# Where a transformer block's vector work is done: keys' weights scaled ahead, key and value blocks made by VectorE alone, and the second norm in two operations over more heads

## The chip, the cores and the metric

The kernel runs on one NeuronCore of a Trainium2 chip. The metric is the device time of one execution in microseconds (us), the median of several runs. A profile of one execution gives each instruction's start and length on TensorE (PE), VectorE (DVE), ScalarE (ACT), GpSimd (POOL) and on SyncE's DMA queue (SP).

## The reference

The program is one transformer block with conditioned layer norms (adaLN), on x of 4 batches x 512 tokens x 512 features, all in fp32:

```python
mod = (silu(c) @ wmod).reshape(4, 6, 1, -1)           # sa, ca, ga, sb, cb, gb
h = layernorm(x) * (1 + ca) + sa
q, k, v = h @ Wq + bq, h @ Wk + bk, h @ Wv + bv       # 16 heads of 128
w = softmax(q @ k.T / sqrt(128) + causal_mask)
x = x + ga * ((w @ v) @ Wo + bo)
h = layernorm(x) * (1 + cb) + sb
x = x + gb * (top2_of_8_experts(h) + shared_expert(h))
```

`ga` and `gb` are kept at least 0.25 away from zero. The change touches the keys and values, and the second layer norm.

## The kernel before, in words

**Products in seven.** The projections of queries, keys, values and the output are 2x2 block products done with seven block multiplications instead of eight (the generator `seven`, L531). Each product goes into a PSUM bank of tag "w", of which there are three, and is taken from there by the engine that the caller names: `p1` (the first product, copied), `11` and `12`, `21`, `22` (the four result blocks), and the running sums `u2`, `u3`, `u4`. If the caller gives a `p5`, the fifth product is first copied to SBUF and the rest works on the copy. The weights' block sums (three more blocks from the four, four additions) are made once, on GpSimd, in batch 0 (`sums_of_a` L505, `sums_of_b` L512) and kept in DRAM (`save_sums` L585). Later batches load two blocks from the input and five from the kept sums (L581, L582).

**Keys** (`project_k`, L654) carry the factor 128^-0.5. Each operation that leaves PSUM applies it. ScalarE takes p1 with the bias (L672), takes the product of u3 with a bias, and copies p5 (L689). GpSimd adds u3 (L679), 22 (L690) and u4 (L692). VectorE does u2, 11, 21 and 12 (all L675). There are 32 key blocks. **Values** (`project_v`, L701): ScalarE copies p1 (L724) and p5 (L727), GpSimd adds 22 (L728) and u4 (L732), VectorE does the rest (L725 to L734). There are 16. **Queries** (`project_q`, L615) take only p1 with ScalarE; all the rest is VectorE's, straight from the bank (L642 to L650).

**Attention.** The work is 16 groups (4 batches b x 4 groups g), four heads u each. In a head, `scores` (L791) makes four blocks of logits: TensorE the products, VectorE the mask (L804) and the negated maximum (L806), ScalarE the exponential (L808), VectorE the reciprocal sums (L812), ScalarE the scaling (L815). `attend` (L817) turns the probabilities with TensorE (L825), copies them out (VectorE L833, ScalarE L835), and multiplies with the values (L839). A head's `scores` are interleaved with the `attend` of the head before.

**The order is written out by hand** for TensorE, VectorE, ScalarE and SP (L1076); each executes in that order and waits where an operand isn't there. GpSimd's order is the planner's. `weave_at` (L1027) runs the eight steps k = 0 to 7 of a head, after each puts in as many steps of `fill` (keys, values, output products) as the head's plan says (L1056 to L1073), and after the steps named in `spots` one step of `side`:

```python
for k, n in enumerate(plan):
    next(main)
    for _ in range(n):
        next(fill)
    if k in spots:
        next(side)
```

**The second norm** (`second_norm`, L964) of batch b-1 is such a side, of 22 steps, run in the heads of batch b's first two groups: four steps of the residual (`xres * ga` on VectorE L234, `+ x` on GpSimd L235); four of statistics (L241, L242), the last with the inverse deviation; four of blocks (subtract and scale L259 on VectorE, `* rows[0]` L276 on VectorE, `+ rows[1]` L277 on GpSimd); then `route` (L308): four steps that turn the blocks with TensorE (L285) and make the router's logits, and six that choose the experts and scatter the rows to DRAM with indirect DMAs on GpSimd (L416). Spots (L1119 to L1125): g = 0: four steps in u1, eight in u2, four in u3; g = 1: three in u0, three in u1. In the last batch (`idle`) ScalarE makes the blocks (L268) after the attention.

**What shares its buffers.** `xres` (the residual and the output projection's sum) has one buffer: `open_out` (L865) fills it with the bias for the next batch at (g, u) = (0, 2), after its old contents went to `xr` in DRAM (L966). `xh` has one buffer: it holds x for the residual and then the second norm's blocks, until the scatter; `load_first` (L858) loads the next batch's x into it at (2, 0), and that batch's first norm (L241, L259) runs at g = 2, u = 2 and 3.

After attention come the shared expert and the routed experts, which the change leaves alone.

Of the kernel before, what the change touches and what calls it, by code (L numbers as in the profile page):

```python
# [8 lines left out]
F32 = mybir.dt.float32  # L9
AF = mybir.ActivationFunctionType  # L10
ALU = mybir.AluOpType
# [3 lines left out]
P = 128  # L15
# [35 lines left out]
def adaln_block_kernel(  # L51
# [64 lines left out]
    for i in range(NT):  # L116
# [26 lines left out]

    sums = {
        "wq": dram.tile([H // 2, P, 5 * 2 * DH], F32, name="sums_q"),
        "wk": dram.tile([H // 2, P, 5 * 2 * DH], F32, name="sums_k"),
        "wv": dram.tile([NG, P, 5 * 4 * DH], F32, name="sums_v"),
        "wo": dram.tile([NG, P, 2 * 6 * HW], F32, name="sums_o"),
        "ws": dram.tile([NSC, P, 7, 2, P], F32, name="sums_s"),
# [74 lines left out]
    def normed(b, n, fine=(1,)):  # L224


        if n == 1:
            src = xh = late["first"]
        else:
            src = xres[b]  # L230
            xh = late["x"]
            rows = late["mod"]
            for t in range(NTB):
                nc.vector.tensor_mul(src[:, t, :], src[:, t, :], ga_bc)  # L234
                nc.gpsimd.tensor_add(src[:, t, :], src[:, t, :], xh[:, t, :])  # L235
                yield
        idle = n == 2 and b == B - 1
        mv = small.tile([P, NTB, 2], F32, tag="mv", name=f"mv_{n}_{b}")
        for t in range(NTB):
            st = small.tile([P, 6], F32, tag="st", name=f"st_{n}_{b}_{t}")  # L240
            nc.vector.bn_stats(st, src[:, t, :])  # L241
            nc.vector.bn_aggr(mv[:, t, :], st)  # L242
            if t in fine:
                yield
        rstd = small.tile([P, NTB], F32, tag="rstd", name=f"rstd_{n}_{b}")
        nc.vector.tensor_scalar_add(rstd, mv[:, :, 1], EPS)
        if idle:
            load_lnexp()
        nc.scalar.activation(rstd, rstd, AF.Ln)
        nc.scalar.activation(rstd, rstd, AF.Exp, scale=-0.5)  # L250
        if idle:
            less = small.tile([P, NTB], F32, tag="less", name=f"less_{n}_{b}")
            nc.vector.scalar_tensor_tensor(
                less, mv[:, :, 0], -1.0, rstd, op0=ALU.mult, op1=ALU.mult
            )
        yield
        for t in range(NTB):
            if not idle:
                nc.vector.tensor_scalar(  # L259
                    xh[:, t, :],  # L260
                    src[:, t, :],
                    mv[:, t, 0:1],
                    rstd[:, t : t + 1],
                    op0=ALU.subtract,
                    op1=ALU.mult,
                )
            else:
                nc.scalar.activation(  # L268
                    xh[:, t, :],
                    src[:, t, :],  # L270
                    AF.Identity,
                    bias=less[:, t : t + 1],
                    scale=rstd[:, t : t + 1],
                )
            if n == 2:
                nc.vector.tensor_mul(xh[:, t, :], xh[:, t, :], rows[0])  # L276
                nc.gpsimd.tensor_add(xh[:, t, :], xh[:, t, :], rows[1])  # L277
            if t in fine:
                yield
        late[b] = xh  # L280
# [291 lines left out]

    def load_quadrants(tag, src, j, b, n=2 * DH, bufs=2):

        w = wts.tile([P, 7, 2, n // 2], F32, tag=tag, bufs=bufs, name=f"{tag}_{b}_{j}")
        flat = w.rearrange("p q c n -> p (q c n)")
        if b == 0:
            nc.sync.dma_start(out=flat[:, : 4 * n], in_=src[j])
            sums_of_a(nc.gpsimd, w)
        else:  # L580
            nc.sync.dma_start(out=flat[:, : 2 * n], in_=src[j, :, : 2 * n])  # L581
            nc.sync.dma_start(out=flat[:, 2 * n :], in_=sums[tag][j])  # L582
        return w

    def save_sums(tag, j, b, w):  # L585
        if b == 0:
            nc.sync.dma_start(
                out=sums[tag][j], in_=w[:, 2:].rearrange("p q c n -> p (q c n)")
            )

    def load_wq(b, j):
# [62 lines left out]
    def project_k(b, i, w, kT):  # L654


        def mm(k, dst):
            sa, sb_ = PROD[k]
            for c in range(2):
                nc.tensor.matmul(  # L660
                    dst,
                    lhsT=w[:, sa, c, :],
                    rhs=h7[b][:, sb_, c, :],
                    start=c == 0,
                    stop=c == 1,
                )

        def out(r, s):
            return kT[:, r, s * HW : (s + 1) * HW]

        def biased(o, p, bias):
            nc.scalar.activation(o, p, AF.Identity, bias=bias, scale=qscale)  # L672

        def add(o, p, u, scale=qscale):
            nc.vector.scalar_tensor_tensor(o, p, scale, u, op0=ALU.mult, op1=ALU.add)  # L675

        def u3(o, p, u):
            biased(o, p, dbk[:, i : i + 1])
            nc.gpsimd.tensor_add(o, o, u)  # L679

        yield from seven(
            f"k_{b}_{i}",
            HW,
            mm,
            {
                "p1": lambda o, p: biased(o, p, sbk[:, 2 * i : 2 * i + 1]),
                "u2": add,
                "u3": u3,
                "p5": lambda o, p: nc.scalar.mul(o, p, qscale),  # L689
                "22": lambda p5, u3: nc.gpsimd.tensor_add(out(1, 1), p5, u3),  # L690
                "21": lambda p, u3: add(out(1, 0), p, u3, -qscale),
                "u4": lambda o, p5, u2: nc.gpsimd.tensor_add(o, p5, u2),  # L692
                "11": lambda p, p1: add(out(0, 0), p, p1),
                "12": lambda p, u4: add(out(0, 1), p, u4),
            },
        )

# [3 lines left out]
    def project_v(b, g, w, v):  # L701


        def mm(k, dst):
            sa, sb_ = PROD[k]
            for t2 in range(2):
                for c in range(2):
                    nc.tensor.matmul(  # L708
                        dst[:, t2 * HW : (t2 + 1) * HW],
                        lhsT=h7[b][:, sb_, c, t2 * P : (t2 + 1) * P],  # L710
                        rhs=w[:, sa, c, :],
                        start=t2 == 0 and c == 0,
                        stop=t2 == 1 and c == 1,
                    )

        def out(r, s):
            return v[:, 2 * s : 2 * s + 2, r * HW : (r + 1) * HW]

        yield from seven(
            f"v_{b}_{g}",  # L720
            S,
            mm,
            {
                "p1": lambda o, p: nc.scalar.copy(o, p),  # L724
                "u2": lambda o, p, u: nc.vector.tensor_add(o, p, u),  # L725
                "u3": lambda o, p, u: nc.vector.tensor_add(o, p, u),
                "p5": lambda o, p: nc.scalar.copy(o, p),  # L727
                "22": lambda p5, u3: nc.gpsimd.tensor_add(  # L728
                    out(1, 1), halves(p5), halves(u3)
                ),  # L730
                "21": lambda p, u3: nc.vector.tensor_sub(out(1, 0), halves(u3), halves(p)),
                "u4": lambda o, p5, u2: nc.gpsimd.tensor_add(o, p5, u2),  # L732
                "11": lambda p, p1: nc.vector.tensor_add(out(0, 0), halves(p), halves(p1)),
                "12": lambda p, u4: nc.vector.tensor_add(out(0, 1), halves(p), halves(u4)),  # L734
            },
        )
# [226 lines left out]

    def second_norm(b):  # L964
        yield from normed(b, 2, (0, 1, 2))
        nc.sync.dma_start(out=xr[b], in_=xres[b].rearrange("p t d -> p (t d)"))  # L966
        yield
        yield from route(b, late[b])

# [106 lines left out]
    with tc.manual_schedule(engines={ENG.PE, ENG.DVE, ENG.Activation, ENG.SP}):  # L1076
# [18 lines left out]
        for G in range(NGB):  # L1095
# [14 lines left out]
            for u in range(GH):  # L1110
# [8 lines left out]
                if g == 0 and b > 0 and u > 0:  # L1119
                    if u == 1:  # L1120
                        second = side = second_norm(b - 1)
                    spots = range(8) if u == 2 else (1, 3, 5, 7)
                elif g == 1 and b > 0 and u < 2:
                    side = second
                    spots = ((1, 3, 5), (1, 3, 7))[u]  # L1125
                elif g == 2 and u >= 2 and b + 1 < B:
                    if u == 2:
                        side = in_order(normed(b + 1, 1))
                    spots = (1, 3)
                elif g == 3 and u == 2 and b + 1 < B:  # L1130
                    side = in_order(quadrants(b + 1))
                    spots = (0, 1, 3, 5)
# [26 lines left out]
                    next(prepare, None)  # L1159

                if b + 1 < B:
                    if (g, u) == (2, 0):
                        load_first(b + 1)
                if (g, u) == (0, 1):
                    wos[G] = load_wo(b, 0)
                if (g, u) == (0, 2 if b > 0 else 1):
                    open_out(b)
                if (g, u) == (3, 2):
                    load_for_second(b)
# [657 lines left out]
```

## Time and profile before

| | |
|---|---|
| runs | 1762.41, 1763.12, 1766.95 us; median 1763.12 |
| the profiled execution | 1764.14 us, span 1762.4 us |
| granted TensorE clock, mean of the span | 0.994 |
| attention and projections | up to about 1240 us of the span |
| DMA | 301.14 MB, mean 171 GB/s |

How to read it. A row of a group has the line, engine, operation, output <- inputs, shape, count, and after the bar busy us and mean ns. A row of waits has who waited for whom, then us in total, times, and the longest. A timeline row has start (us), length (us), engine, line, operation, tiles, shape, count; the bracket is the engine's idle time before it and what ended that. [...] A window row has its length, and then for PE, PEld (weight loads), DVE, ACT and POOL the busy us with the count of instructions, the granted TensorE clock, the share of the DMA engines and GB/s.

The page cuts the span into 40 slices of 44 us; its DMA line has the engines nearly full in batch 0 (from about 110 to 330 us):

```
DMA  5569989736343254334324275615324555565352
```

### The profile page before, as it was taken

Reading aid. Unit: us, or ns where it says so; the run is one execution under the profiler, and the core shown is the slowest. Engines: PE = TensorE matmul, PEld = TensorE weight load, DVE = VectorE, ACT = ScalarE, POOL = GpSimd, SP = SyncE. Lnnn points to the kernel's source line nnn. Section 1 sums busy time; section 2 is a strip of 40 time slices with the busy share of each in tenths; the row PEclk is TensorE's granted clock in tenths of the full one; section 3 lists DMA queues with packets and bytes.
Section 4 is the critical chain, followed back from the end, with each engine's and each line's share of the span. In section 5 each row is a group of like instructions: output and inputs, shape, how many; then the busy total and the mean of one; then the engine's idle time right before and its main releaser. Section 6 shows DMA issues by size and latency. Waiting matters only on the chain. (4 is left out here: it accounts for less than half of the span.)

```text
span 1762.4 us, 21698 instructions
## 1 busy us (share of the span) xinstructions
PE 1701.7 (97%) x7550; PEld 1302.2 (74%) x7550; DVE 896.5 (51%) x1891; ACT 528.5 (30%) x1298; POOL 589.5 (33%) x703
## 2 busy tenths in 40 slices
PE   6999999999999999999999989999999999999998
PEld 4767787787778888688788867787788565655687
DVE  4454454546545455754655475444776232121298
ACT  1025444303453420444441144444320111111120
POOL 6335553314354220525330255533620111000370
PEclk9999999999999999999999999999999999999999
DMA  5569989736343254334324275615324555565352
GB/s 219 184 213 303 281 291 301 261 116 239 94 166 112 84 168 146 124 108 142 110 101 146 96 253 180 196 55 227 126 94 169 215 191 170 193 215 186 110 182 68
DMA packets 158526, 301.14 MB, mean 171 GB/s; under 512 B 19136, under 2 KB 99008, under 8 KB 151760
## 3 DMA queue, kind: packets, MB, share of 16 engines
q1 hardware_dynamic: 153296, 282.96, 47.7%
q0 software_dynamic: 5120, 16.78, 2.9%
q8 instruction: 61, 1.00, 0.2%
q14 instruction: 49, 0.40, 0.1%
HBM read 247.25 MB, written 97.03 MB: 195 GB/s over the span
## 5 line engine op out<-in xcount | busy, mean ns | idle before, releaser
L808 ACT ACTIVATE prob<-ps,nmax 128x128 f32<-128x128 f32 (+3 forms) x256 | 134.4, 525 | 363.2 <-DVE nmax L806 355.6
L660 PE MATMUL w_k<-h,wk 128*128 128x256 f32 x896 | 223.5, 387 | 4.6 <-DVE h L515 2.4
L745 PE MATMUL w_o<-wo,oS 128*128 128x256 f32 x896 | 208.9, 379 | 0.0
L708 PE MATMUL w_v<-wv,h 128*128 128x256 f32 x896 | 206.0, 379 | 1.3 <-DVE u_q L642 1.3
L622 PE MATMUL w_q<-h,wq 128*128 128x256 f32 x896 | 201.9, 380 | 1.8 <-DVE qT L648 1.8
L622 PEld LDWEIGHTS w_q<-h,wq 128*128 128x128 f32 x896 | 168.7, 190 | 27.8 <-issue 3.4
L660 PEld LDWEIGHTS w_k<-h,wk 128*128 128x128 f32 x896 | 165.9, 195 | 27.9 <-ACT p_k L672 5.3
L708 PEld LDWEIGHTS w_v<-wv,h 128*128 128x128 f32 x896 | 167.4, 190 | 22.9 <-DVE u_q L642 1.7
L745 PEld LDWEIGHTS w_o<-wo,oS 128*128 128x128 f32 x896 | 164.6, 190 | 21.3 <-issue 1.4
L797 PE MATMUL ps<-kT,qT 128*128 128x128 f32 (+3 forms) x512 | 173.2, 440 | 1.4 <-ACT prob L808 1.4
L839 PE MATMUL po<-probT,v 128*128 128x512 f32 (+3 forms) x512 | 150.4, 435 | 12.3 <-DVE probT L833 12.3
L839 PEld LDWEIGHTS po<-probT,v 128*128 128x128 f32 x512 | 95.5, 190 | 68.7 <-issue 30.3
L815 ACT ACTIVATE prob<-prob,rsum 128x128 f32<-128x128 f32 (+3 forms) x256 | 122.8, 551 | 63.2 <-DVE rsum L812 61.5
L825 PEld LDWEIGHTS ppt<-ident,prob 128*128 128x128 f32 x640 | 83.3, 143 | 73.4 <-issue 34.7
L758 POOL TENSOR_TENSOR xres<-xres,p_o 128x512 f32<-128x512 f32 x48 | 61.4, 1281 | 209.4 <-DVE xres L758 118.1
L806 DVE TENSOR_REDUCE nmax<-ps 128x1 f32<-128x128 f32 (+3 forms) x256 | 125.7, 491 | 8.8
L1259 PE MATMUL w_s<-h2s,ws 128*128 128x256 f32 x560 | 124.4, 381 | 3.3 <-DVE hid L1245 1.8
L1259 PEld LDWEIGHTS w_s<-h2s,ws 128*128 128x128 f32 x560 | 105.0, 190 | 20.8 <-issue 2.7
L825 PE MATMUL ppt<-ident,prob 128*128 128x128 f32 x640 | 108.4, 278 | 7.6 <-ACT prob L815 5.1
L804 DVE TENSOR_TENSOR ps<-ps,cmask 128x128 f32<-128x128 f32 x256 | 75.1, 293 | 60.4 <-PE ps L797 52.2
L1516 PE MATMUL pyt<-wdn,hTt 128*128 128x512 f32 (+1 forms) x216 | 98.7, 593 | 0.0
L1499 DVE TENSOR_TENSOR ht<-tsg,put 128x352 f32<-128x352 f32 x36 | 18.8, 521 | 147.5 <-PE put L1489 123.0
(281 smaller groups left out, 2348.9 us busy)
## 6 DMA issues: line engine op xcount, KB each, us to landing
wgu<-in_wexp_dram SPq DMA_DIRECT2D x36, 1408.0 KB
xs<-nothing SPq DMA_DIRECT2D x15, 2304.0 KB
wdn<-in_wexp_dram SPq DMA_DIRECT2D x36, 768.0 KB
wo<-sums_o SPq DMA_DIRECT2D x12, 1536.0 KB
wq<-sums_q SPq DMA_DIRECT2D x24, 640.0 KB
wk<-sums_k SPq DMA_DIRECT2D x24, 640.0 KB
wv<-sums_v SPq DMA_DIRECT2D x12, 1280.0 KB
xt<-xs SPq DMA_DIRECT2D x36, 256.0 KB
```

The source lines that it names most:

```text
L622: nc.tensor.matmul(dst, lhsT=w[:, sa, c, :], rhs=h7[b][:, sb_, c, :], start=c == 0, stop=c == 1,)
L660: nc.tensor.matmul(dst, lhsT=w[:, sa, c, :], rhs=h7[b][:, sb_, c, :], start=c == 0, stop=c == 1,)
L708: nc.tensor.matmul(dst[:, t2 * HW : (t2 + 1) * HW], lhsT=h7[b][:, sb_, c, t2 * P : (t2 + 1) * P], rhs=w[:, sa, c, :], start=t2 == 0 and c ...
L745: nc.tensor.matmul(dst[:, t2 * HW : (t2 + 1) * HW], lhsT=oSs[hp][:, sa, t2 * P : (t2 + 1) * P], rhs=w[:, hp, sb_, :], start=t2 == 0 and hp ...
L797: nc.tensor.matmul(ps[:, :n], lhsT=qT[:, q0 : q0 + P], rhs=kT[:, u % 2, :n], start=True, stop=True,)
L806: nc.vector.tensor_reduce(nmax, ps[:, :n], AX.X, ALU.max, negate=True)
L808: nc.scalar.activation(blk, ps[:, :n], AF.Exp, bias=nmax, accum_out=rsum[:, i : i + 1])
L815: nc.scalar.mul(blk, blk, rsum[:, k : k + 1])
L825: nc.tensor.transpose(pt[:, at : at + P], prob[:, QO[i] + j * P : QO[i] + (j + 1) * P], ident,)
L839: nc.tensor.matmul(po[:, j * P :], lhsT=v()[:, j, u * DH : (u + 1) * DH], rhs=probT[:, KO[j] : KO[j] + (NTB - j) * P], start=(j == 0), sto ...
L1259: nc.tensor.matmul(dst[:, n * HW : (n + 1) * HW], lhsT=ws[k][:, sa, c, :], rhs=h2s[b + n][:, sb_, c, :], start=(n == 0 and c == 0), stop=( ...
L1516: nc.tensor.matmul(py, lhsT=hT_t[:fn, k, :], rhs=wdn[i % 2][:fn, k * D : (k + 1) * D], start=(k == 0), stop=(k == len(FCH) - 1),)
```

## The change

What it does:

- The keys' weights are multiplied by 128^-0.5 on GpSimd right after they are loaded in batch 0, ahead of their sums. All seven blocks are kept in DRAM (896 KB for 640 KB), and later batches load them in one DMA.
- Keys are then taken like queries: ScalarE only p1; u2, u3, 22, u4, 21, 11 and 12 on VectorE from the bank. Values have no p5 either: 22 and u4 are VectorE's.
- A block of the second norm (other than the last batch's) is two `scalar_tensor_tensor` on VectorE: (x - mean) * rows[0], then * rstd + rows[1].
- The 22 steps of the second norm are placed otherwise: g = 0: four in u1, two in u2, two in u3; g = 1: four, four, three, three in u0 to u3. The store to `xr` goes out right after the residual's fourth addition. `open_out` moves from (0, 2) to (1, 0), `load_first` from (2, 0) to (2, 1), and the first norm's steps in u2 from k = 1, 3 to k = 5, 7.

```diff
-        "wk": dram.tile([H // 2, P, 5 * 2 * DH], F32, name="sums_k"),
+        "wk": dram.tile([H // 2, P, 7 * 2 * DH], F32, name="sums_k"),
...
                 nc.gpsimd.tensor_add(src[:, t, :], src[:, t, :], xh[:, t, :])
+                if t == NTB - 1 and b < B - 1:
+                    nc.sync.dma_start(out=xr[b], in_=src.rearrange("p t d -> p (t d)"))
                 yield
...
-            if not idle:
+            if n == 1:
                 nc.vector.tensor_scalar(
...
+            elif not idle:
+                nc.vector.scalar_tensor_tensor(
+                    xh[:, t, :],
+                    src[:, t, :],
+                    mv[:, t, 0:1],
+                    rows[0],
+                    op0=ALU.subtract,
+                    op1=ALU.mult,
+                )
+                nc.vector.scalar_tensor_tensor(
+                    xh[:, t, :],
+                    xh[:, t, :],
+                    rstd[:, t : t + 1],
+                    rows[1],
+                    op0=ALU.mult,
+                    op1=ALU.add,
+                )
             else:
...
-            if n == 2:
                 nc.vector.tensor_mul(xh[:, t, :], xh[:, t, :], rows[0])
                 nc.gpsimd.tensor_add(xh[:, t, :], xh[:, t, :], rows[1])
...
             nc.sync.dma_start(out=flat[:, : 4 * n], in_=src[j])
+            if tag == "wk":
+                nc.gpsimd.tensor_scalar_mul(flat[:, : 4 * n], flat[:, : 4 * n], qscale)
             sums_of_a(nc.gpsimd, w)
+        elif tag == "wk":
+            nc.sync.dma_start(out=flat, in_=sums[tag][j])
...
-                "p1": lambda o, p: biased(o, p, sbk[:, 2 * i : 2 * i + 1]),
-                "u2": add,
-                "u3": u3,
-                "p5": lambda o, p: nc.scalar.mul(o, p, qscale),
-                "22": lambda p5, u3: nc.gpsimd.tensor_add(out(1, 1), p5, u3),
-                "21": lambda p, u3: add(out(1, 0), p, u3, -qscale),
-                "u4": lambda o, p5, u2: nc.gpsimd.tensor_add(o, p5, u2),
-                "11": lambda p, p1: add(out(0, 0), p, p1),
-                "12": lambda p, u4: add(out(0, 1), p, u4),
+                "p1": lambda o, p: nc.scalar.activation(o, p, AF.Identity, bias=bias),
+                "u2": lambda o, p, u: nc.vector.tensor_add(o, p, u),
+                "u3": lambda o, p, u: nc.vector.scalar_tensor_tensor(
+                    o, p, d, u, op0=ALU.add, op1=ALU.add
+                ),
+                "22": lambda p, u3: nc.vector.tensor_add(out(1, 1), p, u3),
+                "u4": lambda o, p, u2: nc.vector.tensor_add(o, p, u2),
+                "21": lambda p, u3: nc.vector.tensor_sub(out(1, 0), u3, p),
+                "11": lambda p, p1: nc.vector.tensor_add(out(0, 0), p, p1),
+                "12": lambda p, u4: nc.vector.tensor_add(out(0, 1), p, u4),
...
-                "p5": lambda o, p: nc.scalar.copy(o, p),
-                "22": lambda p5, u3: nc.gpsimd.tensor_add(
-                    out(1, 1), halves(p5), halves(u3)
-                ),
+                "22": lambda p, u3: nc.vector.tensor_add(out(1, 1), halves(p), halves(u3)),
...
-                "u4": lambda o, p5, u2: nc.gpsimd.tensor_add(o, p5, u2),
+                "u4": lambda o, p, u2: nc.vector.tensor_add(o, p, u2),
...
-                    spots = range(8) if u == 2 else (1, 3, 5, 7)
-                elif g == 1 and b > 0 and u < 2:
+                    spots = ((1, 3, 5, 7), (3, 7), (3, 7))[u - 1]
+                elif g == 1 and b > 0:
                     side = second
-                    spots = ((1, 3, 5), (1, 3, 7))[u]
+                    spots = ((1, 3, 5, 7), (1, 3, 5, 7), (1, 3, 5), (1, 3, 7))[u]
...
-                    spots = (1, 3)
+                    spots = ((5, 7), (1, 3))[u - 2]
...
-                    if (g, u) == (2, 0):
+                    if (g, u) == (2, 1):
                         load_first(b + 1)
...
-                if (g, u) == (0, 2 if b > 0 else 1):
+                if (g, u) == ((1, 0) if b > 0 else (0, 1)):
                     open_out(b)
```

## The prediction

> **What bounds the kernel now.** I read the page first, then TensorE's waits, then the timelines of the places where those waits sit, then clock by window, then mean durations by shape.
>
> ```profile
> PE 1701.7 (97%) x7550; PEld 1302.2 (74%) x7550; DVE 896.5 (51%) x1891; ACT 528.5 (30%) x1298; POOL 589.5 (33%) x703
> ```
>
> TensorE is busy 1701.7 of 1762.4 us. The change leaves its instructions alone, so all it can win is the 60.7 us of idle time plus matmuls that ran at a lower clock. TensorE's waits:
>
> ```profile
> PE po L839 <- DVE probT L833: 12.3, 6, 2.7
> PE pln L285 <- POOL xh L277: 5.5, 6, 1.6
> PE ppt L825 <- ACT prob L815: 5.1, 13, 1.5
> PE w_k L660 <- ACT p_k L672: 2.2, 5, 0.5
> ```
>
> TensorE's timeline puts most of these 30 gaps in a few places. Three times, once a batch, it looks like this (last batch; the bracket is the idle time before the row):
>
> ```profile
> 1031.39 0.92 PE L839 MATMUL po<-probT,v 128*128 128x256 f32 x4 [2.69 <-DVE probT L833]
> 1037.30 0.33 PE L285 MATMUL pln<-ident,xh 128*128 128x128 f32 x1 [0.16 <-POOL xh L277]
> 1039.19 0.36 PE L285 MATMUL pln<-ident,xh 128*128 128x128 f32 x1 [1.56 <-POOL xh L277]
> ```
>
> VectorE and GpSimd in that place:
>
> ```profile
> 1028.85 0.89 DVE L259 TENSOR_SCALAR xh<-xres,mv,rstd 128x512 f32<-128x512 f32 x1
> 1029.77 1.10 DVE L276 TENSOR_TENSOR xh<-xh,rows 128x512 f32<-128x512 f32 x1
> 1030.79 0.55 DVE L833 COPY probT<-ppt 128x384 f32<-128x384 f32 x1
> ...
> 1036.16 1.64 DVE L276 TENSOR_TENSOR xh<-xh,rows 128x512 f32<-128x512 f32 x1
> ...
> 1037.87 1.26 POOL L277 TENSOR_TENSOR xh<-xh,rows 128x512 f32<-128x512 f32 x1 [0.62 <-DVE xh L276]
> ```
>
> Eight steps of the second norm in one head (u2) put its statistics and blocks ahead of that head's transposed-probability copy (L833); VectorE is 98% busy in 1030 to 1040, TensorE 69%. The clock drops just there:
>
> ```profile
> 1020.00:1030.00 10.00, 8.63 (x40) 5.87 (x39) 9.10 (x25) 6.14 (x18) 5.63 (x6) 1.00 0.97 368
> 1030.00:1040.00 10.00, 6.89 (x26) 4.96 (x27) 9.75 (x15) 4.03 (x12) 8.04 (x8) 0.80 0.82 325
> 1040.00:1050.00 10.00, 10.00 (x57) 7.89 (x56) 3.29 (x9) 5.57 (x13) 6.16 (x9) 0.86 0.71 232
> ```
>
> The second place is the keys' block. GpSimd is in order, and the keys' additions queue behind whatever it has; VectorE waits for them, and the softmax behind VectorE:
>
> ```profile
> 209.84 0.73 POOL L690 TENSOR_TENSOR kT<-p_k,u_k 128x256 f32<-128x256 f32 x1
> 210.52 0.73 POOL L692 TENSOR_TENSOR p_k<-p_k,u_k 128x256 f32<-128x256 f32 x1
> ...
> 211.28 0.42 DVE L675 SCALAR_TENSOR_TENSOR kT<-w_k,p_k 128x256 f32<-128x256 f32 x1 [3.23 <-POOL p_k L692]
> 211.63 0.17 DVE L812 RECIPROCAL rsum<-rsum 128x4 f32<-128x4 f32 x1
> ...
> 211.83 1.92 ACT L815 ACTIVATE prob<-prob,rsum 128x128 f32<-128x128 f32 x4 [3.42 <-DVE rsum L812]
> ...
> 212.28 0.73 PE L825 MATMUL ppt<-ident,prob 128*128 128x128 f32 x2 [0.74 <-ACT prob L815]
> ```
>
> Here the keys' sums had waited behind four sums of wo (204.2 to 209.9).
>
> **Part 1: keys and values on VectorE.** GpSimd loses 24.6 + 24.2 + 23.4 us (keys: L692, L679, L690) and 20.3 + 20.3 (values: L732, L728). ScalarE loses 15.1 (u3) + 12.6 (p5) + 9.4 (values' p5) = 37 us. VectorE gains per key block what the queries' rows of the same shape cost: u3 0.48 (L643), u4 0.40 (L647), 22 about 0.42 = 1.30 us, x32 = 42 us; per value block 2 x 0.69 (L725) = 1.38, x16 = 22 us. The four key operations it had stay near 0.42. [...] The bank is held for two operations instead of one copy (0.8 for 0.4 us in keys); three banks rotate, product time 0.86 us, so it is covered.
>
> What falls away is GpSimd's delay. Gaps that the timeline ties to it: 1.88 at 143 us, 1.75 at 212 to 216, 2.63 at 271 to 277, 1.95 at 336 to 338, 1.76 at 1112: **10.0 us, of which I count 9** (some of ScalarE's softmax backlog stays). Next late there is ScalarE's p1, whose waits at 326, 626 and 922 (0.37 each) stay.
>
> **Part 2: scaling the keys' weights.** Eight GpSimd multiplications 128x1024, no row like it. Below: a memset 32x2048 took 1.80 us, so 0.9; above: twice the two-input 128x512 addition, 2.5. I take 1.7, 14 us in all. No PE wait names these sums. At the start two come before use: wk's sums ended at 17.0 us and TensorE needs them after 24.8; wq's ended at 25.6 and the first is needed at 35.4. Even 5 us later is covered. In batch 0 each save grows from 640 to 896 KB, 2.1 MB in all, 7 us of transfer at 295 GB/s where DMA is 99% busy. SP waits for it before reloading wk, but a reload issued at 212 is used some 45 us later. Zero; without cover, up to 7. Later batches load the same bytes in one DMA instead of two: nothing.
>
> **Part 3: the norm's block.** Before: L259 0.58 and L276 1.40 (0.69 free, 1.64 beside GpSimd's L277), then L277 1.41 on GpSimd. After: two operations of two SBUF tensors and a scalar. Bounds 0.69 (free) and 1.64 (contended); nearest row L1563, 0.75, so 1.5 us a block. VectorE saves 12 x 0.5 = 6 us, GpSimd 17, and the waits on L277 have no source left.
>
> **Part 4: the spreading.** The order of the 22 steps stays; head u2 gets 2 instead of 8, both statistics. Gone should be 6.5 us of waits for L833 (1.93 + 1.92 + 2.69), 5.5 for L277 and 0.9 of the transposes at 440: **12.9, I count 12**. The lower clock: 10 us windows at 0.83 (440), 0.98 and 0.85 (726, 736), 0.80 and 0.86 (1030, 1040) cost 1.7 + 1.7 + 3.4 = **6.8 us**. [...] The rows show the dips, but only where several gaps come within 10 us; the lone 1.9 to 2.1 us gaps at 143 and 271 have clock 1.00. As the gaps go, so should the dips: I take 6.8.
>
> New costs. (a) Head g1 u0 now holds a key block and four norm blocks. Nearest: the head at 858, with a key block and first-norm blocks (1.87 and 0.91 us of VectorE before the copy). Its L833 copy ended at 868.47, TensorE could use it from 869.19. The new head has 3.0 of norm for 2.78, 1.07 more of keys (start to start), less 0.41 that VectorE idled: 869.35, 0.2 late; with contended norm operations up to 3.5. I take 0.7 x 3 = 2. (b) The head at 858 itself gets 1.07: 0.5 x 3 = 1.5. (c) load_first one head later: SP now issues it behind wv (837.6). 1.8 + 1.0 MB at 300 GB/s land near 848; the statistics moved to about 854. Free, but in batch 0, where DMA is full and sums_o (1.5 MB) goes first, near 255 against 253.5; behind that wait stand rsum and the next masks: 1.5 (0 to 5). (d) Values' VectorE work beside the modulation rows (stalls at 62 and 110 us): 0.7. (e) xr's store, now ahead of wo on SP, waits for the last L235 (727): wo 4 us later, needed 50 us on; the bias load of xres at about 766 instead of 740, needed at 786: zero. The h2 stores queue after it. Route's steps in heads g1 u1 to u3: 0.3. Scatter's 8 us on GpSimd moves to g1 u3, after the output block instead of into it: zero. **Sum 6 us (0 to 17).**
>
> **The sum.** 9 + 12 + 6.8 - 6 = 21.8 us. The profiled execution took 1764.14 with span 1762.4, 1.7 outside; the median of the three runs is 1763.12. 1763.1 - 21.8 = 1741.3; I say 1742. VectorE should go to about 954 us (54%).
>
> **Rivals.** *The stall only moves*: cost (a) at its contended end, 3.5 x 3 = 10.5 instead of 2, and at most half of the clock term won. Then 21.8 - 8.5 - (3.4 to 6.8) = 6.5 to 9.9: 1753 to 1757. For it: that head is nearly full. Against: GpSimd has no norm or key work left there. *No change*: full DMA in batch 0 (7) and a late x (3.5 more) as well, and the boundaries' 12 us half won: within 5 of 1763. *VectorE becomes the bound*, which ends slower: it gets 64 us more work, in order, in heads where the softmax hangs on it. It decides where a block's additions push L833 past TensorE's second matmul on it, a margin of 0.7 us in the head at 858. If all 48 blocks do and TensorE loses 1.2 us on each (the 1.38 of a value block less fill), that is 58 us, less the 27.8 won: 1793. Against: a key head then has 3.0 + 4.5 us of VectorE work (softmax rows L804, L806, L812, L833) beside 12.8 of TensorE, so only bursts could do it. *The change doesn't act as said*: GpSimd, ordered by the planner, could put the multiplications ahead of L235, on which the statistics wait; at most 1.7 us each in batch 0, where there is no second norm: no different from the forecast.
>
> **Chances.** Likeliest case 1733 to 1750: 0.60. Stall moves, 1750 to 1757.8: 0.22. No change (within 0.3%, about what a measurement can tell): 0.09. Slower: 0.09. Range 1733 (all 29.7 won) to 1758.
>
> **What would show it.** Right: no PE wait on POOL L277; PE's wait for L833 at most 4 us; no VectorE wait for POOL in key blocks; clock 1.00 near 440, 736, 1035; PE idle about 40. Wrong: a wait for L833 in head g1 u0, VectorE waiting for xh's DMA near 254, TensorE waiting for wk's bank on VectorE.

## The result, and the profile after

The changed kernel takes 1737.12 us (median of 4 runs, 1735.93 to 1738.17) against 1762.83 us for the kernel before (4 runs, 1762.41 to 1766.95): a ratio of 0.9854, 95% interval 0.9843 to 0.9866. That is 25.7 us won; the forecast was 1742, 21.8 us won, with a range of 1733 to 1758. The profiled execution took 1736.06 us with a span of 1734.4, so it is 28.1 us shorter than that of before.

In the changed file the lines have moved: the probability copy is L846, the value product L852, the transposes of probabilities L838, the keys' products L684, p1 of the keys L701, the other key operations L702 to L710, the norm's two operations L270 and L278, the scaling of the weights L599. The page's first row, after:

```profile
PE 1691.5 (98%) x7550; PEld 1298.3 (75%) x7550; DVE 943.5 (54%) x2019; ACT 495.0 (29%) x1218; POOL 487.9 (28%) x571
```

TensorE's idle time fell from 60.7 to 42.9 us. Its busy time fell by 10.2 us with the same 7550 instructions. By the clock records 19.9 us of the span were at half speed before and 7.2 after, start and end included, which makes up 6.4 of the 10.2; I have no cause for the rest. VectorE took on 47 us of work, and GpSimd lost 102. TensorE's waits, after (who for whom, us in total, times, longest):

```profile
PE w_k L684 <- ACT p_k L701: 5.8, 7, 1.9
PE po L852 <- DVE probT L846: 3.0, 4, 1.0
...
PE ppt L838 <- ACT prob L828: 1.0, 4, 0.3
```

The 12.3 us for the probability copy became 3.0, the 5.5 for GpSimd's addition are gone, the 5.1 for ScalarE's probabilities became 1.0. One row grew: 2.2 us for the keys' p1 became 5.8. The timeline of TensorE and VectorE in head (1, 0) of the last batch, which now has the norm blocks (the counterpart of the 2.69 us gap shown of before):

```profile
1026.17 0.41 DVE L706 TENSOR_TENSOR kT<-w_k,u_k 128x256 f32<-128x256 f32 x1
1026.50 0.41 DVE L707 TENSOR_TENSOR p_k<-w_k,u_k 128x256 f32<-128x256 f32 x1
...
1027.16 0.74 DVE L270 SCALAR_TENSOR_TENSOR xh<-xres,mv,rows 128x512 f32<-128x512 f32 x1
1027.94 0.75 DVE L278 SCALAR_TENSOR_TENSOR xh<-xh,rstd,rows 128x512 f32<-128x512 f32 x1
...
1030.14 0.92 PE L852 MATMUL po<-probT,v 128*128 128x256 f32 x4 [0.66 <-DVE probT L846]
```

VectorE goes through the key block (22, then u4) without waiting for anybody, makes one norm block in 1.5 us, and TensorE is held up for 0.66 us: cost (a), forecast at 0.7. And by 10 us window (TensorE busy first; the clock is third from the end):

```profile
1010.00:1020.00 10.00, 9.98 (x49) 7.41 (x48) 8.38 (x24) 6.24 (x17) 5.60 (x8) 1.00 1.00 367
1020.00:1030.00 10.00, 9.48 (x42) 6.57 (x40) 7.90 (x17) 3.39 (x12) 3.00 (x5) 1.00 0.78 267
1030.00:1040.00 10.00, 9.86 (x50) 8.75 (x51) 6.76 (x13) 4.42 (x12) 7.55 (x9) 1.00 0.69 246
```

The clock is 1.00 where it was 0.80 and 0.86.

To say where the time went I made a table from the traces. For each two neighbouring TensorE instructions, the time from start to start is compared with the usual one for the first's line and shape (the 40th percentile); what is over is summed by head. That counts gaps and slow clock alike. Before minus after is 28.1 us, just the difference of the two profiled executions. (Lost us; (g, u) is group and head; b1-3 are batches 1 to 3; the runs are told below.)

```
place                         before  after    e1    e2    e8    e9    e5   e12
before the first head           16.5   12.4  15.0  13.3  13.7  14.5  13.6  17.3
batch 0 without (2,3)           12.5    3.5   3.5  14.1  14.3   5.1   3.5   9.7
(0,2) (0,3) (1,1), b1-3         26.0    0.8  21.5   9.3   1.0   1.0   0.8   5.7
(1,0), b1-3                      0.4    3.6   0.4   2.7   4.1   4.1   3.9  13.6
(1,3), b1-3                      2.0    2.9   0.0   3.7   2.6   2.6   2.9   3.6
(2,0) to (2,2), b1-3             0.1    0.1   0.1   8.6   2.0   4.6   2.9   0.6
(2,3), all batches               2.4    8.3   1.5   9.2   7.0   7.7   2.4  11.6
other heads                      3.3    3.6   3.3   3.6   3.6   3.6   3.6   6.5
last head and all after         16.8   16.8  15.8  15.6  16.1  15.0  17.0  15.8
sum                             80.0   51.9  61.2  80.0  64.4  58.2  50.6  84.5
```

Each column is one execution. The first row is partly chance: e2 and the next two runs (e3, e4) have the start of the kernel before and lost 13.3 to 14.7 us there, where the profiled execution of before lost 16.5; the runs with the start of the changed kernel (e1, e5, e6, e7, e11) lost 11.9 to 15.0. Batch 0 varies too where the keys are GpSimd's: 12.5 us before, 14.1, 18.1 and 13.4 in e2, e3 and e4, of which e3 changes nothing there, and the others only the place of the first norm and its load.

### The profile page after: what moved, and what is told of

Same layout as the page of the kernel before. It is cut to its first block, busy times and chain, and to the rows that moved or that the text cites. A ratio compares the mean times of both kernels' runs of the same rounds, so it can differ in the third digit from the quotient of the medians.

```text
span 1734.4 us, 21464 instructions
## 1 busy us (share of the span) xinstructions
PE 1691.5 (98%) x7550; PEld 1298.3 (75%) x7550; DVE 943.5 (54%) x2019; ACT 495.0 (29%) x1218; POOL 487.9 (28%) x571
## 5 line engine op out<-in xcount | busy, mean ns | idle before, releaser
L684 PE MATMUL w_k<-h,wk 128*128 128x256 f32 x896 | 220.9, 383 | 7.9 <-ACT p_k L701 5.8
L684 PEld LDWEIGHTS w_k<-h,wk 128*128 128x128 f32 x896 | 162.1, 191 | 32.4 <-ACT p_k L701 11.4
L852 PE MATMUL po<-probT,v 128*128 128x512 f32 (+3 forms) x512 | 152.2, 438 | 3.1 <-DVE probT L846 3.0
L852 PEld LDWEIGHTS po<-probT,v 128*128 128x128 f32 x512 | 96.2, 192 | 60.3 <-issue 30.8
L838 PEld LDWEIGHTS ppt<-ident,prob 128*128 128x128 f32 x640 | 82.1, 141 | 63.8 <-issue 34.0
L838 PE MATMUL ppt<-ident,prob 128*128 128x128 f32 x640 | 104.0, 275 | 2.9 <-ACT prob L828 1.0
L817 DVE TENSOR_TENSOR ps<-ps,cmask 128x128 f32<-128x128 f32 x256 | 75.2, 294 | 55.7 <-PE ps L810 47.8
```

The lines of the kernel that those rows point to most:

```text
L684: nc.tensor.matmul(dst, lhsT=w[:, sa, c, :], rhs=h7[b][:, sb_, c, :], start=c == 0, stop=c == 1,)
L838: nc.tensor.transpose(pt[:, at : at + P], prob[:, QO[i] + j * P : QO[i] + (j + 1) * P], ident,)
L852: nc.tensor.matmul(po[:, j * P :], lhsT=v()[:, j, u * DH : (u + 1) * DH], rhs=probT[:, KO[j] : KO[j] + (NTB - j) * P], start=(j == 0), sto ...
```

## The experiments

Times are medians. Ratios are to the kernel before on the same chip, with the 95% interval in brackets; its medians there are 1763.58 to 1764.39 us, so where a difference is small the ratios say more than the times.

**The halves by themselves.** Theory: the terms of the forecast are separate and add up. Rival: the stall moves, so that a half by itself gives less (or more) than its terms.

e1, keys and values alone: the hunks for `sums`, `load_quadrants`, `save_sums`, `project_k` and `project_v`; the second norm as before.

> Kernel before with parts 1 and 2 alone (keys' weights scaled ahead, keys and values on VectorE); the second norm and its places as before. Theory (the forecast's term): the boundary gaps at 143, 212, 271, 336 and 1112 go (9 us), the three places near 440, 735 and 1035 with their waits for L833 and L277 and their low clock stay: 1755 (1752 to 1758). Rival (the stall only moves): with the keys' work beside the eight norm steps, the wait for the transposed-probability copy grows past 12.3 us in sum and eats half: 1759 or more. TensorE's busy time stays near 1701.

Measured: 1746.07 us, ratio 0.9907 (0.9888 to 0.9927), some 16 us won, about twice the term. The batch 0 row gained its 9.0 us and head (1,3) of the last batch 2.0, which is the term. The surprise is the third row, 26.0 to 21.5. The waits for the probability copy in the three crowded heads shrank only from 1.93, 1.92 and 2.69 us to 1.59, 1.59 and 2.53, so the burst is a little milder; but of the four half-speed stretches (near 445, 735, 1032 and 1039 before) two went, 3.4 us, though the gaps of 1.56 us at the transposes stayed. The last section says why the same gaps need not bring the same clock. TensorE's busy time was 1694.4, not 1701.

e2, the second norm alone: the hunks for `normed`, `second_norm`, `spots`, `load_first` and `open_out`; keys and values as before.

> Kernel before with parts 3 and 4 alone (two-operation block, second norm over more heads, first norm's steps and load_first later); keys and values as before. Theory: 12 us of gaps and 6.8 of clock won, 4 lost to the first norm's new place: 1748 (1745 to 1752), TensorE's busy time near 1693, clock 1.00 near 440, 735 and 1035. Rival (the clock term is not tied to these gaps): 1755 with busy time still near 1700. If the two halves of the change don't overlap, this gain and that of the keys-and-values run add up to 25.7 us.

Measured: 1766.21 us, ratio 1.0013 (1.0005 to 1.0020): nothing won, if anything 2 us lost. Both expectations failed, and so does the sum of the terms: 2.3 us slower here and 16 faster in e1 don't make 25.7. The heads from which the norm was taken did gain 16.7 us (third row), but everything below and batch 0 lost as much. Where it went shows in the timeline of e2 in head (2,0) of the last batch (L434 is the scatter, L697 the keys' u3 addition, L693 VectorE's key operation, L857 the value product):

```profile
1118.99 0.96 POOL L434 DMA_INDIRECT xs<-xh,slots  x1 [0.30 <-issue]
...
1119.97 0.73 POOL L697 TENSOR_TENSOR u_k<-u_k,u_k 128x256 f32<-128x256 f32 x1
1120.73 0.42 DVE L693 SCALAR_TENSOR_TENSOR kT<-w_k,u_k 128x256 f32<-128x256 f32 x1 [6.16 <-POOL u_k L697]
...
1122.61 1.55 PE L857 MATMUL po<-probT,v 128*128 128x256 f32 x4 [3.35 <-DVE probT L851]
```

Read it from below: TensorE waits for the probability copy, VectorE had stood 6.16 us before a key block's result, because GpSimd's addition for it came after the last of eight scatter DMAs, which with four small additions among them had held GpSimd since 1107.99. The spread moved the scatter past the norm's old place, to where a key block is next. In the changed kernel the same scatter stands at 1083.5 to 1095.5 and nobody waits for it.

e3, the two-operation block alone, and e4, the spread alone with the old block of three operations:

> Kernel before with part 3 alone: the second norm's block in two VectorE operations, placed as before. Theory: the 5.5 us of waits for the GpSimd addition go, VectorE's burst is some 0.5 us a block shorter, so 1 us of the wait for the probability copy goes too; the low clock stays in good part: 1756 (1753 to 1759). Rival: the burst alone makes the stall, nothing won: 1761 to 1763. Other rival: the clock dips came from the transposes that waited for GpSimd, and go with them: 1750.

> Kernel before with part 4 alone: the old block of three operations (GpSimd still adds), spread over more heads, first norm and load_first later. Theory: the burst is gone, so 6.5 us of waits for the probability copy, most of 6.8 of clock and, as route's transposes now follow the last block a head later, 5 of the waits for GpSimd; 4 to 5 lost at the first norm's new place: 1750 (1746 to 1754). Rival: the old blocks' GpSimd additions now stand beside the keys' GpSimd additions of head g = 1, u = 0, and VectorE waits for GpSimd there: 1756 or more.

Measured: e3 1759.16 us, ratio 0.9976 (0.9968 to 0.9984), 4.2 us won, just past the weak end of its theory: the waits for GpSimd's addition went, but the wait for the probability copy was 15.2 us in its trace and not below 12.3. Of that 3.6 is one wait in batch 0 (1.9 before), where e3's instructions are those of before: the load of `wo` came 1.4 us later, and with it its sums on GpSimd and the key additions behind them. e4 1765.80 us, ratio 1.0010 (1.0002 to 1.0019): the number is its rival's, but not the cause. The rival blamed the old block's GpSimd additions in head (1,0). e2 hasn't got them and loses the same as e4 in every row to within 1.3 us, in (2,0) to (2,2) 8.6 and 8.5, so in both it is the scatter ahead of the key additions. Without the keys' part the spread is worth nothing, with the old block or the new.

**The first norm's place.** In the changed kernel 8.3 us are lost in heads (2,3). The timeline of batch 1 there:

```profile
547.70 0.41 DVE L248 TENSOR_SCALAR rstd<-mv 128x4 f32<-128x4 f32 x1
...
548.02 0.28 DVE L817 TENSOR_TENSOR ps<-ps,cmask 128x128 f32<-128x128 f32 x1
...
549.80 0.47 ACT L701 ACTIVATE p_k<-w_k,sbk 128x256 f32<-128x256 f32 x1
...
550.32 1.13 PE L684 MATMUL w_k<-h,wk 128*128 128x256 f32 x4 [1.31 <-ACT p_k L701]
```

The statistics, now after the last step of head u2, stand ahead of the next head's masks (L817); the exponentials wait for those, ScalarE's p1 stands behind the exponentials, and TensorE needs p1's bank. In batch 0 VectorE also waited 1.49 us for the DMA of `xh` (247.55), and TensorE 1.87 us (254.78). e5 puts both back:

```diff
-                    spots = ((5, 7), (1, 3))[u - 2]
+                    spots = (1, 3)
...
-                    if (g, u) == (2, 1):
+                    if (g, u) == (2, 0):
                         load_first(b + 1)
```

> Changed kernel, with the next batch's first norm and its load put back where they were (load_first after head (2, 0), steps of u2 after k = 1 and 3). Theory: the later place costs 1.6 us in head (2, 3) of batches 1 and 2 and 3.6 in batch 0, so 6.8 us come back: 1730 (1728 to 1733), and TensorE's wait for ScalarE's p1 falls from 5.8 to about 1.1 us. Rival: the load, now issued while GpSimd still scatters from the same buffer, holds up SP and the weights behind it, and the gain is lost again: 1736 or more, with TensorE or VectorE waiting for a DMA in group 2.

Measured: 1731.55 us, ratio 0.9812 (0.9798 to 0.9825), an interval clear of the change's: 5.6 us faster than the changed kernel by the medians, 7 by the ratios, and the lowest median of all. Heads (2,3) fell to 2.4 us lost; 2.8 us were newly lost in (2,0) to (2,2). TensorE's wait for p1 in e5:

```profile
PE w_k L684 <- ACT p_k L701: 1.4, 4, 0.4
```

The rival did not come true: neither TensorE nor VectorE waits for a DMA in group 2.

e6, two norm steps more in head (0,2) and two fewer in (1,0), and e7, e5 and e6 together; e11, as e7 with the two blocks of head (0,3) placed otherwise:

```diff
 e6:
-                    spots = ((1, 3, 5, 7), (3, 7), (3, 7))[u - 1]
+                    spots = ((1, 3, 5, 7), (1, 3, 5, 7), (3, 7))[u - 1]
...
-                    spots = ((1, 3, 5, 7), (1, 3, 5, 7), (1, 3, 5), (1, 3, 7))[u]
+                    spots = ((3, 7), (1, 3, 5, 7), (1, 3, 5), (1, 3, 7))[u]
 e11 against e7:
-                    spots = ((1, 3, 5, 7), (1, 3, 5, 7), (3, 7))[u - 1]
+                    spots = ((1, 3, 5, 7), (1, 3, 5, 7), (1, 7))[u - 1]
```

> Changed kernel, with two more second-norm steps in head (0, 2) (four instead of two) and two fewer in head (1, 0), which has the full key block. Theory (cost (a) of the forecast): head (1, 0) loses 1.2 us in each of three batches and gets nearly all of it back: 1734 (1732 to 1736). Rival: the four statistics now stall head (0, 2) by as much: 1737. In head (0, 3) two norm blocks stand beside part of a key block: if that stalls, 1739 or more.

> The two edits of place together (first norm back, second norm two steps earlier). Theory: they touch different heads, so the gains add up: 6.8 + 3 us, 1727 (1725 to 1730), the fastest of all. Rival: one of them gives nothing, then as the other alone: 1730 or 1734.

> As the run with both places moved (e7), but the two norm blocks of head (0, 3) after k = 1 and 7 instead of 3 and 7. There the block after k = 3 stood ahead of the head's last mask and last probability copy, 1.3 us in batches 1 and 2 and 2.2 in batch 3. Theory: these 4.8 us come back: 1729 (1727 to 1732), the fastest. Rival: the block after k = 1 pushes the later copies just as far: 1734.

Measured: e6 1738.46 us, ratio 0.9859 (0.9844 to 0.9874), nothing won over the change. Head (1,0) went from 3.6 to 0.2 us lost, and head (0,3) lost 4.3 more: the stall only moved. e7 1734.14 us, ratio 0.9829 (0.9816 to 0.9843): the gain of e5 and none beside it. e11 1733.00 us, ratio 0.9823 (0.9806 to 0.9839): its trace, of its fastest execution, lost 46.0 us, the least of all, and 3.8 in the third row where e7's lost 5.6. But the medians of e5, e7 and e11 can't be told apart, so the expected 1729 is not shown.

**What covers GpSimd's scaling.** e8 is the changed kernel with the values made as before (p5 copied by ScalarE, two additions on GpSimd):

> Changed kernel, with the values made as before (p5 copied by ScalarE, 22 and u4 added by GpSimd), keys and second norm changed. Theory: no stall that went was tied to a value block, and what the spread needs is that keys leave GpSimd: 1737 (1735 to 1739), VectorE busy some 20 us less. Rival: the values' additions queue behind GpSimd's scatter or weight sums as the keys' did: 1741 or more, with VectorE waiting for GpSimd in value blocks. Other rival: the values on VectorE cost something: 1733 or less.

Measured: 1748.63 us, ratio 0.9910 (0.9896 to 0.9924). The theory was wrong by 11 us, the rival right. Timeline of e8 in head (1,1) of batch 0:

```profile
169.52 2.77 POOL L599 TENSOR_SCALAR wk<-wk 128x1024 f32<-128x1024 f32 x1 [7.46 <-DMA wk<-in_wk_dram]
...
176.45 1.26 POOL L748 TENSOR_TENSOR p_v<-p_v,u_v 128x512 f32<-128x512 f32 x1
...
177.75 0.69 DVE L750 TENSOR_TENSOR v<-w_v,p_v 128x512 f32<-128x512 f32 x1 [6.89 <-POOL p_v L748]
...
179.88 1.65 PE L855 MATMUL po<-probT,v 128*128 128x256 f32 x4 [3.48 <-DVE probT L849]
```

The chain is that of e2 with other names: a scaling and four sums of the next `wk` block stand ahead of a value block's additions, VectorE waits 6.89 us, TensorE 3.48. e9 leaves the scaling out of e8:

```diff
-            if tag == "wk":
-                nc.gpsimd.tensor_scalar_mul(flat[:, : 4 * n], flat[:, : 4 * n], qscale)
```

> The kernel with values made as before (e8), with the scaling of the keys' weights left out: its logits lack the factor 128^-0.5, so that part of the computation is missing; every other instruction is the same. In e8 the values' additions on GpSimd waited behind a scaling of 2.77 us and four sums of wk, in heads (1, 1) and (2, 1) of batch 0, 5.3 and 4.7 us lost. Theory (the scaling costs nothing only because values have left GpSimd): without it these two heads lose less than 3 us together, and the time is near 1739 (1737 to 1742). Rival (the sums of wk alone, or another of GpSimd's queues, make that stall): 1745 or more, with VectorE's wait for GpSimd's p_v still near 19 us.

Measured: 1742.24 us, ratio 0.9867 (0.9848 to 0.9887). The two heads lost 0.3 us together instead of 10.0, so the scaling did make that stall. The time did not quite come to 1739 (VectorE still waited 11.8 us for GpSimd's part of the value blocks, and (2,0) to (2,2) lost 4.6), and its interval overlaps that of the changed kernel. e10 doubles the scaling in the changed kernel:

```diff
-                nc.gpsimd.tensor_scalar_mul(flat[:, : 4 * n], flat[:, : 4 * n], qscale)
+                nc.gpsimd.tensor_scalar_mul(flat[:, : 4 * n], flat[:, : 4 * n], qscale**0.5)
+                nc.gpsimd.tensor_scalar_mul(flat[:, : 4 * n], flat[:, : 4 * n], qscale**0.5)
```

> Changed kernel, the keys' weights multiplied twice by the root of the factor: 2.8 us more on GpSimd for each of eight blocks, all in batch 0. Theory (nothing waits for GpSimd any more in these heads): 1737 (1736 to 1739). Rival (the scaling is only just covered, by the time to wk's use or to wq's first sums): 1740 to 1748, with TensorE waiting for wk or wq at the start or in batch 0.

Measured: 1743.17 us, ratio 0.9877 (0.9858 to 0.9896), 6 us over the change's median and 4 by the ratios; the two intervals overlap, so a loss is likely but not certain. One longer wait is in the trace of e10:

```profile
42.08 0.33 SPq L612 DMA_DIRECT2D sums_v<-wv  x1
...
42.98 0.95 SPq L597 DMA_DIRECT2D wq<-in_wq_dram  x1
...
52.50 1.75 PE L647 MATMUL w_q<-h,wq 128*128 128x256 f32 x7 [3.47 <-DMA wq<-in_wq_dram]
```

In SP's order this load stands behind the save of wv's sums, which went out at 42.08; in the changed kernel GpSimd ended those sums at 38.02, the save went out at 38.04 and the wq load at 39.92, and TensorE had no such wait. The load came 3.1 us later and TensorE waited 3.5, so hardly any cover was left at the start. e5, whose start is the changed kernel's, has the same wait already, with 0.88 us. What else e10 lost lies in small differences that I can't tie to the scaling.

**The fifth product copied first.** The changed kernel's 22 and u4 read the fifth product from its bank. In the kernel before, a 128x512 addition on VectorE took 0.692 us from PSUM and SBUF (L725, median of 16) and 0.692 from SBUF alone (L1378, median of 8). In e12 ScalarE copies the fifth product of keys and values to SBUF, and VectorE's 22 and u4, two operations, read the copy (the lines shown are the keys'; the values' are changed alike).

```diff
+                "p5": lambda o, p: nc.scalar.copy(o, p),
-                "22": lambda p, u3: nc.vector.tensor_add(out(1, 1), p, u3),
+                "22": lambda p5, u3: nc.vector.tensor_add(out(1, 1), p5, u3),
```

> Changed kernel, with the fifth product of keys and values first copied out of PSUM by ScalarE, and VectorE's 22 and u4 reading the copy. By the rows of the trace VectorE's duration does not change (0.42 and 0.69 us) and ScalarE gets 22 us more: 1737 (1736 to 1740), VectorE busy 943. [...] Rival: the copies stand in ScalarE's queue beside the exponentials and delay p1 and the probabilities: 1742 or more.

Measured: 1764.55 us, ratio 0.9999 (0.9987 to 1.0012): the whole gain is gone. VectorE was busy 951.2 us, 7.7 more than in the changed kernel. Two of VectorE's waits in e12, the second new:

```profile
DVE kT L710 <- ACT p_k L701: 40.2, 27, 2.0
DVE kT L707 <- ACT p_k L706: 38.7, 30, 1.4
```

VectorE, in order, stands 1.3 us in 30 of 32 key blocks before ScalarE's copy, which stands behind an exponential and a probability copy; for the values it is another 24.3 us in 16. What follows in VectorE's queue are the next masks and the probability copy, and TensorE's wait for that went from 3.0 to 17.1 us (14 times); half-speed stretches came back (four places). By the table most of it was lost in head (1,0), 10.0 us more than in the changed kernel, and in batch 0, 6.2. Some of VectorE's additions also took longer (last section); e12 does not separate that from the waits.

## Why the prediction was right, and where its steps were not

The time was inside the range and 4.9 us below the forecast. The mechanism was right: GpSimd's queue and the crowded head made the stalls, and with both gone most of that idle time and the low clock there went. What failed is that the terms stand alone and add up. The sizes were off on both sides and partly cancelled, so that the sum came within 5 us is in part luck.

**Keys and values (9 us).** The batch 0 row and the last batch's 1112 us gap gave 9.0 + 2.0. The durations were right: u3 0.482, u4 0.414, 22 0.420 (forecast 0.48, 0.40, 0.42), the values' pair 0.689 + 0.680 (1.38). What the term missed by itself is the 4.5 us of the third row in e1 (26.0 to 21.5), of which two half-speed stretches are 3.4. Part of the 9.0 hangs on the one trace of before: e2, e3 and e4 lost up to 5.6 more in batch 0.

**The spread and the clock (12 + 6.8 us).** Heads (0,2), (0,3), (1,1) gave 25.2 us, of them 20.7 on top of e1. The clock half is confirmed: the four half-speed stretches near 445, 735, 1032 and 1039 are gone. Two others stand at 256.00, behind the late first norm of (2,3), and at 1198.08, so during attention two are gone on balance. That the spread is a gain by itself was the failed step: alone it lost 2 us (e2) instead of winning 12 + 6.8 less the new costs. The prediction put "Scatter's 8 us on GpSimd moves to g1 u3, after the output block instead of into it: zero": zero it is only with the keys off GpSimd. The rival *the stall only moves* did not come true for the change, but is what e2 and e4 do.

**Scaling the weights (zero).** In the changed kernel's trace nothing waits for it, though no run leaves the scaling out there; its size and the reason for its cover were wrong. The row, after:

```profile
L599 POOL TENSOR_SCALAR wk<-wk 128x1024 f32<-128x1024 f32 x8 | 22.2, 2771 | 53.1 <-DMA wk<-in_wk_dram 45.1 <-PE ppt L838 5.9 <-issue 1.9
```

2.77 us, above my upper bound of 2.5, which took one input of twice the length to be no dearer than two two-input additions of half of it. I had named TensorE's use of the weights and the reload of wk as what covers it. The runs showed two other conditions: that no value block needs GpSimd behind it (e8, 10 us), and the order of SP's saves at the start: "even 5 us later is covered" held for the changed kernel, where wv's sums end at 38.0 instead of 31.8 us, but for 0.88 us in e5; another 4 us (e10) were not covered.

**The norm's block (0.75 an operation).** 0.742 and 0.752 us in the 8 of 12 where GpSimd was idle, 0.978 and 1.097 in the 4 beside it. VectorE came to 943.5 us, not 954: with less beside it on GpSimd its other work is shorter too. The first norm's block went from 0.815 to 0.651 us in the mean: it takes 0.54 alone in both kernels, but 10 of 16 stood beside GpSimd before and 2 after. The residual's multiplication went from 0.894 to 0.790.

**The new costs (6 us).** They were 12. (a) 3.2 for 2 in head (1,0). (b) and (c), the head at 858 and the late load, 5.9 for 3: I had looked at the probability copy there, and the wait came by p1's bank. Route's steps in heads (1,3) lost 2.9, forecast at 0.3 (the 2.0 lost there before were the gap at 1112, counted above). Of the 5.9, 1.7 is the half-speed stretch at 256.00. (d), the values beside the modulation rows, did not appear: those stalls are 1.12, 0.95 and 1.50 us after, and 1.29, 1.14 and 1.81 before.

So by the table, 11.0 + 25.2 − 12 = 24 us, and 4.1 at the start, of which some 2 to 3 are chance; the medians say 25.7, the forecast 21.8.

## What to carry to other kernels

Work that stood ahead in GpSimd's queue held up TensorE by 3.35 us in e2 and 3.48 in e8, so two edits that each move work past the same queue can't be costed apart: here one gave 0.9%, the other nothing, both together 1.5%. When steps are spread over more places, list for each engine what is next in its queue at every new place, not only at the place that was relieved. In e12 the copy of the fifth product, behind an exponential and a probability copy in ScalarE's queue, was a new wait: 1.3 us in 30 of 32 key blocks.

## What the hardware showed

**The low clock comes in fixed pieces.** All half-speed stretches in these traces' attention are 3.41 us long or twice that, and within a trace they start on one grid: in the kernel before at 445.45, 735.58, 1032.54 and 1039.37, which lie 290.13, 296.96 and 6.83 us apart, 85.0, 87.0 and 2.0 times the 3.413 us of one record. A TensorE that is busy throughout such a piece loses half of it by the record's 0.50, an estimated 1.7 us. I counted TensorE's idle share in each piece of that grid during attention, in all traces. Of 32 half-speed pieces 27 follow a piece that was idle for half of it or more. Every piece idle for over 0.58 was followed by half speed, and five idle for 0.52 to 0.58 were not. The other five half-speed pieces follow pieces idle for 0.31 to 0.39, so the share alone is not the whole rule. One gap of 1.87 us did it (it ends at 254.78 in the changed kernel, half speed from 256.00), as did gaps of 0.33 and 1.56 us together (before, half speed from 445.45), while a gap of 1.88 us that lies across two pieces (it ends at 143.13, before) did not.

The same gaps can come out either way. Near 337 us the kernel before and e3 have the same three, of 1.49, 0.18 and 0.28 us (e3: 1.48, 0.18, 0.28), but the grid cuts them differently. First two pieces of before, then two of e3:

```profile
332.81:336.23 3.42, 1.93 (x10) 1.29 (x8) 0.51 (x2) 0.72 (x3) 2.12 (x3) 1.00 0.98 299
336.23:339.64 3.41, 2.88 (x14) 2.21 (x14) 1.35 (x3) 2.13 (x5) 0.00 (x0) 1.00 1.14 343
...
336.71:340.13 3.42, 1.66 (x7) 1.04 (x8) 0.82 (x3) 2.65 (x6) 0.20 (x1) 1.00 1.15 343
340.13:343.54 3.41, 3.41 (x10) 2.70 (x9) 1.40 (x3) 0.20 (x1) 0.00 (x0) 0.50 1.11 368
```

In e3 one piece holds 1.76 us of the idle time, and the next runs at half speed; in before it is split into 1.49 and 0.53, and the clock stays. So how many such pieces a run gets is in part chance. None of the pieces ahead of half speed in before and after was idle throughout: before 0.55, 0.56, 0.66 and 0.50, after 0.55 and 0.31. "Several gaps within 10 us" in the prediction was near it, but not the rule.

**VectorE beside GpSimd.** Here is the keys' 22 in e12, with both inputs in SBUF, and in the changed kernel, with one in PSUM (shortest, median and longest in ns):

```profile
L707 DVE TENSOR_TENSOR kT<-p_k,u_k x32: 424/426/1497, 33.2 to 1183.5; 128x256 f32<-128x256 f32 x32
...
L706 DVE TENSOR_TENSOR kT<-w_k,u_k x32: 411/423/426, 30.4 to 1148.7; 128x256 f32<-128x256 f32 x32
```

With both inputs in SBUF it took 0.43 us where GpSimd was idle (21 of 32), and 0.81 in the mean and up to 1.50 where it was working (u4: 0.42, 0.99 and 1.49). With one input in PSUM it took 0.42 either way (13 of 32 beside GpSimd). So for these additions the copy to SBUF made VectorE slower beside GpSimd, and no faster alone.
